# The router's weights as the stationary operand in four column quarters, and a block transpose on VectorE

## The chip, the cores and the metric

The kernel runs on one core of a Trainium2 chip. TensorE multiplies, ScalarE and VectorE work on its results, GpSimd and SyncE issue transfers beside what else they do. The metric is the device time of one execution in microseconds; for the kernel before, it is the median of three runs.

## What is computed

One block of a transformer over 16 sequences of 100 tokens with 256 channels: cross-attention to a context of 361 rows with 16 heads of 64, then a mixture of experts. Only the router is touched by the change, so it is shown in full and the rest in outline:

```python
x = x + cross_attention(layernorm(x), ctx)           # Wq, Wkv, Wproj, bproj
h = layernorm(x)                                     # 1600 tokens x 256
logits = clip(h @ router_w.T + routing_bias, -50, 50)   # router_w: 7 x 256
probs = sigmoid(logits)
p, sel = top_k(probs, 1)                             # one of 7 experts for each token
p = clip(p, 1e-8, 1 - 1e-8)
total = clip(0.5 + p + 1e-8, 0.5, 2.0)
shared = swiglu(h, sw1, sw2, sw3)                    # 704 hidden units
switched = p * swiglu(h, ew1[sel], ew2[sel], ew3[sel])
x = x + 0.5 / total * shared + switched / total
```

Everything is in float32.

## The kernel before

The 1600 tokens lie in 13 tiles of 128 (the last holds 64). `acc` holds them token by token, 128 tokens on the partitions; `xT` holds the normalised tokens turned, 128 channels on the partitions and two halves `k` of the 256 channels, so that matmuls can contract over channels. The tiles are handled in four `GROUPS` of 3, 3, 3 and 4 tiles.

**Attention** (L454 to L848) runs in 32 steps, two for each sequence, 8 heads in each. A step computes scores (L618), their maxima and exponentials, turns the exponentials in blocks of 32 on VectorE (L647), moves the blocks by DMA (L668), and multiplies with the values of the step before (L689). Between the scores stand the products of keys and values for the next sequence (L551), the queries (L527, emptied by VectorE on L534) and the projection (L716). The order of TensorE is written out by hand everywhere; that of ScalarE, VectorE and SyncE is so within the attention, and left to a planner outside it. GpSimd's order is the planner's.

When all tokens of a group are through the attention, the group's norm is computed, its `xT` is made by TensorE transposes (L202, copied on L205), and its router follows. This is done through queues of small parts: `part()` takes one part from `norms` at a time between other work, and `fillers` puts `router(g)` in. So the first three calls of the router, each for 3 tiles, lie inside the attention: behind a step's scores and ahead of query matmuls. The fourth call, for 4 tiles, stands behind the attention, between the second matmuls of the shared expert (`down`, L445 and L448) for one tile and for the next two.

**The router** has, for every tile and each half `k`, one matmul (L232): the 128x128 block of `xT` is the stationary operand and the router's weights, 128 channels by 7 experts, stream through. The logits come out token by token, in one PSUM bank for the whole group, as `lp[token, tile, expert]`. VectorE adds the bias (L246), which takes them out of PSUM, and some twenty small operations give the chosen expert (`onehot`, L273), its probability and the weights of the two sums.

**Behind the fourth call** `sort_tokens` (L294) places every token in a slot of an expert's tile of 128. Its two matmuls (L299, L300) read `onehot`. While VectorE does the sorting, TensorE computes the shared expert's hidden units (L402) for the other groups. Then each expert tile is gathered, multiplied (L920, L929, L941) and scattered to the output; the experts' weights, 2.2 MB a tile, are fetched up to four tiles ahead.

PSUM is used as eight banks of 128x512 that `bank()` hands out in turn. The router's weights `rw_sb` and bias `rb_sb` are loaded in step 3 (L496, L497), far ahead of their first use.

Of the kernel before, what the change touches and what calls it, by code (L numbers as in the profile page):

```python
# [14 lines left out]
F32 = mybir.dt.float32  # L15
# [3 lines left out]
ALU = mybir.AluOpType  # L19
# [6 lines left out]
I, E = 704, 7  # L26
P = 128
# [27 lines left out]
def xattn_moe(  # L55
# [16 lines left out]
    nc = tc.nc  # L72
# [4 lines left out]
    const = ctx.enter_context(tc.tile_pool(name="const", bufs=1))  # L77
    small = ctx.enter_context(tc.tile_pool(name="small", bufs=2))
# [6 lines left out]
    xT = const.tile([P, 2, NT * P], F32, name="xT")  # L85
# [1 line left out]
    ident = const.tile([P, P], F32, name="ident")  # L87
    power = const.tile([P, 4], F32, name="power")
    rank = const.tile([P, E], F32, name="rank")
    rw_sb = const.tile([P, 2, E], F32, name="rw_sb")  # L90
    rb_sb = const.tile([P, E], F32, name="rb_sb")
    bp_sb = const.tile([P, C], F32, name="bp_sb")
    onehot = const.tile([P, NT, E], F32, name="onehot")
# [21 lines left out]
    def bank():  # L115
        return ps.tile([P, 512], F32, tag="mm", name="mm")
# [10 lines left out]
    def load_x(g):  # L127
        full = [t for t in g if t < NT - 1]
        t0, n = full[0], len(full)
        nc.sync.dma_start(  # L130
            acc[:, t0 : t0 + n, :],
            x[t0 * P : (t0 + n) * P, :].rearrange("(t p) c -> p t c", p=P),
        )
        if g[-1] == NT - 1:
            nc.sync.dma_start(acc[:LAST, NT - 1, :], x[(NT - 1) * P :, :])

    make_identity(nc, ident)
    nc.gpsimd.memset(power, -0.5)
    for e in range(E):
        nc.gpsimd.memset(rank[:, e : e + 1], float(E - e))  # L140
        nc.gpsimd.memset(tri[:, e, :], 0.0)
        if e:
            nc.gpsimd.memset(tri[:, e, :e], 1.0)
# [69 lines left out]
    def load_shared(i):  # L213

        if i < 4:
            k, o = i // 2, ds(i % 2 * I, I)
            nc.sync.dma_start(w13_sb[:, k, o], w13[ts(k, P), o])
        elif i == 4:
            nc.sync.dma_start(w2_sb[:, :3, :], w2[: 3 * P].rearrange("(i p) c -> p i c", p=P))
        else:  # L220
            r = w2[3 * P : NI * P].rearrange("(i p) c -> p i c", p=P)
            nc.sync.dma_start(w2_sb[:, 3:NI, :], r)
            nc.sync.dma_start(w2_sb[P - HALF :, NI, :], w2[NI * P :])

    def router(tiles):


        t0, n = tiles[0], len(tiles)
        lp = bank()[:, : 4 * E].rearrange("p (t e) -> p t e", e=E)
        for i, t in enumerate(tiles):  # L230
            for k in range(2):
                nc.tensor.matmul(  # L232
                    lp[:, i, :], xT[:, k, ts(t, P)], rw_sb[:, k, :], start=(k == 0), stop=(k == 1)
                )

        def over_experts(a):
            return a[:, :n].unsqueeze(2).to_broadcast([P, n, E])

        lg = small.tile([P, 4, E], F32, name="lg")
        pr = small.tile([P, 4, E], F32, name="pr")  # L240
        eq = small.tile([P, 4, E], F32, name="eq")
        sat = small.tile([P, 4, E], F32, name="sat")
        top = small.tile([P, 4], F32, name="top")
        tw = small.tile([P, 4], F32, name="tw")
        bias = rb_sb.unsqueeze(1).to_broadcast([P, n, E])
        nc.vector.tensor_tensor(lg[:, :n], lp[:, :n], bias, ALU.add)  # L246
        lmax = small.tile([P, 4], F32, name="lmax")

        def odds():
            nc.vector.tensor_scalar(lg[:, :n], lg[:, :n], -50.0, 50.0, ALU.max, ALU.min)  # L250
            nc.scalar.activation(pr[:, :n], lg[:, :n], AF.Exp, scale=-1.0)
            nc.vector.tensor_scalar(pr[:, :n], pr[:, :n], 1.0, None, ALU.add)
            nc.vector.reciprocal(pr[:, :n], pr[:, :n])

        def best():


            nc.vector.tensor_reduce(top[:, :n], pr[:, :n], AX.X, ALU.max)
            nc.vector.tensor_tensor(eq[:, :n], pr[:, :n], over_experts(top), ALU.is_equal)
            nc.vector.tensor_scalar(sat[:, :n], lg[:, :n], 6.0, None, ALU.is_gt)  # L260
            nc.vector.tensor_tensor(sat[:, :n], sat[:, :n], eq[:, :n], ALU.mult)

        def first():
            nc.vector.tensor_reduce(lmax[:, :n], lg[:, :n], AX.X, ALU.max)
            nc.vector.tensor_tensor(eq[:, :n], lg[:, :n], over_experts(lmax), ALU.is_equal)
            nc.vector.tensor_tensor(eq[:, :n], eq[:, :n], sat[:, :n], ALU.max)
            nc.vector.tensor_tensor(
                eq[:, :n], eq[:, :n], rank.unsqueeze(1).to_broadcast([P, n, E]), ALU.mult
            )
            nc.vector.tensor_reduce(lmax[:, :n], eq[:, :n], AX.X, ALU.max)  # L270

        def chosen():
            nc.vector.tensor_tensor(  # L273
                onehot[:, t0 : t0 + n, :], eq[:, :n], over_experts(lmax), ALU.is_equal
            )
            if tiles[-1] == NT - 1:
                nc.vector.memset(onehot[LAST:, NT - 1, :], 0.0)

        def weights():

            nc.vector.tensor_scalar(top[:, :n], top[:, :n], 1e-8, 1.0 - 1e-8, ALU.max, ALU.min)
            nc.vector.tensor_scalar(tw[:, :n], top[:, :n], 0.5, 1e-8, ALU.add, ALU.add)
            nc.vector.tensor_scalar(tw[:, :n], tw[:, :n], 0.5, 2.0, ALU.max, ALU.min)
            nc.vector.reciprocal(tw[:, :n], tw[:, :n])
            nc.vector.tensor_scalar(coef[:, t0 : t0 + n], tw[:, :n], 0.5, None, ALU.mult)
            nc.vector.tensor_tensor(
                entry[:, t0 : t0 + n, 1], top[:, :n], tw[:, :n], ALU.mult
            )
            if tiles[-1] == NT - 1:
                nc.vector.memset(entry[LAST:, NT - 1, :], 0.0)  # L290

        return [odds, best, first, chosen, weights]
# [161 lines left out]
    with ExitStack() as attn:  # L454
# [33 lines left out]
        def load_later(s):  # L488

            if 1 < s < 4:  # L490
                m = ts(s - 2, NCH // 2)
                nc.sync.dma_start(
                    wp_sb[:, m], wproj.rearrange("(m p) c -> p m c", p=P)[:, m]
                )
            if s == 3:
                nc.sync.dma_start(rb_sb, rbias.to_broadcast([P, E]))  # L496
                nc.sync.dma_start(rw_sb, rwT.rearrange("(k p) e -> p k e", p=P))  # L497
            if s == 4 or s == 7:
                load_x(GROUPS[s // 3 + 1])
            if s == 6 or s == 9:  # L500
                normalised(GROUPS[s // 3])
            if 10 <= s < 16:
                load_shared(s - 10)
# [221 lines left out]
        def normalised(g, keep=False):  # L725
            parts, turn = layer_norm(g, keep)
            norms.extend(parts)
            norms.append(lambda: turns.append(turn))
            if keep:
                norms.append(lambda: fillers.append(lambda: norms.extend(router(g))))  # L730
# [49 lines left out]
        for s, (b, g) in enumerate(steps):  # L780
# [51 lines left out]
            if g == NG - 1 and b + 2 < B:  # L832
                cTs[b + 2] = load_ctx(b + 2)
            load_later(s)
        while first:
            first.pop(0)()
# [51 lines left out]
    with tc.tile_pool(name="hs", bufs=1) as hs:  # L888
        def run_hidden(g):
            n = sum(map(rows, g))  # L890
            hT = hs.tile([P, NI + 1, n], F32, name=f"hT{n}")
            for piece in hidden(g, hT, sp):
                piece()
            return hT

        parts, turn_last = layer_norm(GROUPS[-1], keep=True)
        for one in parts:
            one()
        hT = run_hidden(GROUPS[1])
        turn_last()  # L900
        down(GROUPS[1][:1], hT)
        for one in router(GROUPS[-1]):
            one()
        down(GROUPS[1][1:], hT[:, :, P:])
        fill = sort_tokens(hs)
        for k in range(NW):
            fetch(k)
        hT2 = run_hidden(GROUPS[2])
        fill()
        for k in range(NX - 1):  # L910
            gather_into(xgs, xn_d, k)
        hT3 = run_hidden(GROUPS[3])
        down(GROUPS[2], hT2)
        down(GROUPS[3], hT3)
# [72 lines left out]
    n = nc.values_load(e_at[:, NS:], min_val=0, max_val=NS - NF)  # L987
# [58 lines left out]
```

## Time and profile before

| | |
|---|---|
| median of 3 runs | 731.54 us (731.47 to 731.96) |
| the profiled execution | 730.98 us |
| its span, first to last instruction | 729.3 us |
| granted TensorE clock, mean | 0.998 |
| router matmuls (L232) | 52 matmul records and 52 weight loads, 205.1 to 548.9 us |
| bias addition (L246) | 4 times, 143 to 188 ns |
| load of the router's weights (L497) | issued on SP at 80.9 us |

The profile was taken on one execution. Its engines are PE (TensorE's matmuls), PEld (its weight loads, which overlap the matmuls), DVE (VectorE), ACT (ScalarE), POOL (GpSimd) and SP (SyncE). A line of a group reads: source line, engine, operation, result<-operands, shapes, count, busy time in us and mean ns of one, and the idle time of the engine ahead of it. A line of the timeline has start and length in us in front, and the idle time with its releaser in brackets. A line of a wait reads: who waited <- for whom, us in all, times, longest. A matmul's end is modelled, so its length is not the time after which the next one can start; that is read from the starts.

### The profile page before, as it was taken

The page shows a single profiled execution, that of the slowest core. Times are in us where ns is not written, and L with a number is a line of the kernel's source. Part 1 is how long each engine was busy: PE and PEld are TensorE (multiplying, and loading weights), DVE is VectorE, ACT ScalarE, POOL GpSimd, SP SyncE. Part 2 cuts the span into 40 slices and gives each one's busy share as a digit, 9 for nine tenths or more (in the row PEclk, how much of TensorE's full clock was granted, in tenths as well). Part 3 has the DMA queues.
Part 4 walks back from the last instruction along what each step waited for, and adds up shares of the span by engine and source line. Part 5 has one row for each costly group of instructions (what it writes and reads, how often), then busy time and mean ns, then how long its engine had stood idle before and what let it go on. Part 6 is the DMA issues. An engine that isn't in the chain of part 4 may idle for free. (4 is left out here: it accounts for less than half of the span.)

```text
span 729.3 us, 14750 instructions
## 1 busy us (share of the span) xinstructions
PE 721.5 (99%) x5206; PEld 516.7 (71%) x5206; DVE 421.2 (58%) x1086; ACT 280.3 (38%) x795; POOL 201.7 (28%) x418
## 2 busy tenths in 40 slices
PE   9999999999999999999999999999999999999996
PEld 6667666676666767576676666756767678999996
DVE  2877668568786866857866695776247222222221
ACT  2554556344544544534534463453021101112111
POOL 5242322323323222422223322223020102543221
PEclk9999999999999999999999999999999999999999
DMA  7164655534655553644534554445103901888860
GB/s 256 47 153 113 178 138 134 129 98 127 174 148 126 147 134 85 162 111 126 137 85 126 119 157 111 109 97 121 58 26 109 419 32 48 317 334 344 308 255 23
DMA packets 54375, 107.95 MB, mean 148 GB/s; under 512 B 28631, under 2 KB 35930, under 8 KB 52368
## 3 DMA queue, kind: packets, MB, share of 16 engines
q1 hardware_dynamic: 43648, 80.51, 36.4%
q0 software_dynamic: 10352, 25.98, 14.2%
q8 instruction: 44, 0.72, 0.4%
q14 instruction: 43, 0.35, 0.2%
q10 hardware_dynamic: 288, 0.39, 0.2%
HBM read 60.39 MB, written 5.35 MB: 90 GB/s over the span
## 5 line engine op out<-in xcount | busy, mean ns | idle before, releaser
L634 ACT ACTIVATE at<-mm,nm 128x361 f32<-128x361 f32 x256 | 142.1, 561 | 206.8 <-DVE nm L631 206.6
L668 POOL DMA_DIRECT2D aT<-tb x256 | 126.4, 501 | 300.1 <-PE mm L689 168.4
L631 DVE TENSOR_REDUCE nm<-mm 128x1 f32<-128x361 f32 x256 | 124.0, 526 | 50.9 <-PE mm L618 49.7
L647 DVE STREAM_TRANSPOSE tb<-at 128x384 f32<-128x384 f32 x256 | 132.9, 558 | 4.8 <-DMA aT<-tb 0.6
L551 PE MATMUL mm<-wv_sb,cT 64*128 64x512 f32 (+1 forms) x576 | 131.6, 589 | 0.0
L551 PE MATMUL mm<-cT,wk_sb 64*128 64x361 f32 x768 | 128.4, 465 | 0.0
L551 PEld LDWEIGHTS mm<-cT,wk_sb 64*128 64x128 f32 x768 | 76.3, 188 | 41.4 <-issue 0.5
L618 PE MATMUL mm<-kT,qT 64*128 64x361 f32 x512 | 103.1, 478 | 0.0
L551 PEld LDWEIGHTS mm<-wv_sb,cT 64*128 64x128 f32 (+1 forms) x576 | 53.9, 181 | 57.3 <-issue 46.5
L929 PE MATMUL mm<-xgT,wex 128*128 128x128 f32 x660 | 78.3, 275 | 0.5 <-ACT xgT L922 0.5
L929 PEld LDWEIGHTS mm<-xgT,wex 128*128 128x128 f32 x660 | 76.9, 192 | 1.4 <-issue 0.7
L689 PEld LDWEIGHTS mm<-aT,v 128*64 128x64 f32 (+1 forms) x1536 | 68.9, 135 | 10.6 <-issue 10.6
L689 PE MATMUL mm<-aT,v 128*64 128x100 f32 (+1 forms) x1536 | 75.2, 252 | 0.0
L618 PEld LDWEIGHTS mm<-kT,qT 64*128 64x128 f32 x512 | 46.6, 185 | 38.7 <-issue 14.4
L402 PE MATMUL mm<-xT,w_sb 128*128 128x384 f32 (+1 forms) x176 | 60.9, 503 | 0.0
L402 PEld LDWEIGHTS mm<-xT,w_sb 128*128 128x128 f32 x176 | 32.9, 190 | 25.7 <-issue 8.5
L634 ACT ACTIVATION_READ_ACCUMULATOR at<-mm,nm 128x1 f32 x256 | 50.4, 197 | 0.0
L527 PE MATMUL mm<-xT,wq_sb 128*128 128x200 f32 x256 | 47.2, 337 | 0.7 <-ACT xT L205 0.7
L716 PE MATMUL mm<-wp_sb,resT 128*128 128x256 f32 (+1 forms) x208 | 47.8, 383 | 0.0
L527 PEld LDWEIGHTS mm<-xT,wq_sb 128*128 128x128 f32 x256 | 43.0, 190 | 4.7 <-issue 2.0
L716 PEld LDWEIGHTS mm<-wp_sb,resT 128*128 128x128 f32 (+1 forms) x208 | 37.7, 186 | 9.9 <-ACT at L634 2.5
L941 PE MATMUL mm<-wex,hgT 128*128 128x256 f32 x180 | 41.4, 380 | 0.0
(139 smaller groups left out, 555.2 us busy)
## 6 DMA issues: line engine op xcount, KB each, us to landing
wex<-in_wex SPq DMA_DIRECT2D x15, 2176.0 KB
aT<-tb POOLq DMA_DIRECT2D x256, 80.2 KB, 3.1
aT<-tb SPq DMA_DIRECT2D x256, 80.2 KB
cT<-in_ctxT SPq DMA_DIRECT2D x15, 541.5 KB
over<-row SPq DMA_DIRECT2D x64, 100.0 KB
xn_d<-xn SPq DMA_DIRECT2D x12, 128.0 KB
base_d<-acc SPq DMA_DIRECT2D x12, 128.0 KB
w_sb<-in_w SPq DMA_DIRECT2D x4, 352.0 KB
```

Source lines behind the costliest of these rows:

```text
L402: nc.tensor.matmul(to[:, :n], w13_sb[:, k, ds(at, P)], xT[:, k, ds(g[0] * P, n)], start=(k == 0), stop=(k == 1),)
L527: nc.tensor.matmul(pq[:, o, :], wq_sb[:, u, k, ts(o, P)], xT[:, k, ts(g, QG * LQ)], start=(k == 0), stop=(k == 1),)
L551: nc.tensor.matmul(to[o][:height, :width], *operands(o, k), start=(k == 0), stop=(k == NR - 1),)
L618: nc.tensor.matmul(sc[o][:, :LKV], qTs[b // QG][r, c, ts(b % QG, QB), :], kTs[b][c // 4][r, c % 4, :], start=True, stop=True,)
L631: nc.vector.tensor_reduce(nm[:, o : o + 1], sc[o][:, :LKV], AX.X, ALU.max, negate=True)
L634: nc.scalar.activation(at[:, o, :LKV], sc[o][:, :LKV], AF.Exp, bias=nm[:, o : o + 1], accum_out=sums[:, o : o + 1],)
L647: nc.vector.transpose(tb[:, :, :, o, i * QR : i * QR + 32].rearrange("p j k n -> p k j n"), at[:, o, :].rearrange("p (k j n) -> p k j n", ...
L668: queue.dma_start(aT[ts(j, 32), i].rearrange("p k o n -> p (k o n)"), tb[ts(i, 32), j].rearrange("p k o n -> p (k o n)"),)
L689: nc.tensor.matmul(av[ts(o, DK), i, :], vs[b][:n, j, ds((2 * c + o) * DK, DK)], aT[:n, :, j, o, ts(i, QR)], start=(j == 0), stop=(j == NJ ...
L716: nc.tensor.matmul(pp[:r, :C], resT[:, c, QP : QP + r], wp_sb[:, c, :], start=(c == 0), stop=(c == NCH - 1))
L929: nc.tensor.matmul(to[:, ts(o, P)], w[:, ds(j * 2 * I + u, P)], xgT[:, j, :], start=(j == 0), stop=(j == 1),)
L941: nc.tensor.matmul(y[:, :C], hT[:, c, :], w[:, ds(4 * I + c * C, C)], start=(c == 0), stop=(c == NI))
```

## The change

The operands of the router's matmuls change places. The weights, padded with zeros from 7 to 32 columns (`rw_sb` is cleared by GpSimd at the start and then loaded in part), become the stationary operand, and the tokens run through. For each half `k` there are four matmuls, one for each `q`: the q-th runs of 32 tokens of all tiles of the group are streamed (96 columns, or 128 in the last call) and the result goes to the 32 PSUM partitions from 32q on, so that each matmul lies in another quarter of the array's columns. Now the logits stand expert by expert: in quarter q, expert e on partition 32q + e, tokens along the row. One VectorE transpose in blocks of 32 out of PSUM puts them back token by token into a new SBUF tile `lp`, of which the bias addition reads the first 7 of each 32. What follows is as before.

```diff
-    rw_sb = const.tile([P, 2, E], F32, name="rw_sb")
+    rw_sb = const.tile([P, 2, 32], F32, name="rw_sb")
...
     nc.gpsimd.memset(power, -0.5)
+    nc.gpsimd.memset(rw_sb, 0.0)
...
         t0, n = tiles[0], len(tiles)
-        lp = bank()[:, : 4 * E].rearrange("p (t e) -> p t e", e=E)
-        for i, t in enumerate(tiles):
-            for k in range(2):
+
+        lt = bank()[:, : n * 32]
+        for k in range(2):
+            of = xT[:, k, ds(t0 * P, n * P)].rearrange("p (t q r) -> p q t r", q=4, r=32)
+            for q in range(4):
                 nc.tensor.matmul(
-                    lp[:, i, :], xT[:, k, ts(t, P)], rw_sb[:, k, :], start=(k == 0), stop=(k == 1)
-                )
+                    lt[ts(q, 32), :].rearrange("p (t r) -> p t r", r=32),
+                    rw_sb[:, k, :],
+                    of[:, q],
+                    start=(k == 0),
+                    stop=(k == 1),
+                )
+
+        lp = small.tile([P, 4, 32], F32, name="lp")
+        nc.vector.transpose(lp[:, :n].rearrange("p t e -> p (t e)"), lt)
...
-        nc.vector.tensor_tensor(lg[:, :n], lp[:, :n], bias, ALU.add)
+        nc.vector.tensor_tensor(lg[:, :n], lp[:, :n, :E], bias, ALU.add)
...
-                nc.sync.dma_start(rw_sb, rwT.rearrange("(k p) e -> p k e", p=P))
+                nc.sync.dma_start(rw_sb[:, :, :E], rwT.rearrange("(k p) e -> p k e", p=P))
```

## The prediction

> **What bounds the kernel now.** I read the busy times first, then what the matmul engine waited for, then the groups of the router's line, then the timeline around each router call.
>
> ```profile
> PE 721.5 (99%) x5206; PEld 516.7 (71%) x5206; DVE 421.2 (58%) x1086; ACT 280.3 (38%) x795; POOL 201.7 (28%) x418
> ```
>
> Busy matmuls alone prove little, because their ends are modelled. The waits of PE settle it: these three are all of them, 2.3 us in 729.3.
>
> ```profile
> PE mm L122 <- DVE ones L119: 1.1, 1, 1.1
> PE mm L527 <- ACT xT L205: 0.7, 1, 0.7
> PE mm L929 <- ACT xgT L922: 0.5, 1, 0.5
> ```
>
> So TensorE is the path from start to end, and time taken off its stream comes off the end unless a wait behind it opens. The first question is how much of that stream the router holds. The windows on its line are the stretches from its first matmul to the first matmul of the next line: us, PE busy (instructions), PEld busy (instructions).
>
> ```profile
> 205.13:206.49 1.36, 1.36 (x12) 1.36 (x12) 1.00 0.76 302
> 333.27:334.63 1.36, 1.36 (x12) 1.36 (x12) 1.00 0.09 35
> 456.74:458.10 1.36, 1.36 (x12) 1.36 (x12) 1.00 0.15 57
> 547.30:549.01 1.71, 1.70 (x16) 1.70 (x15) 1.00 0.08 29
> ```
>
> Four calls, 5.79 us at full clock. Each f32 matmul of the source shows as two passes, each with its weight load: 26 matmuls, 52 passes, 111 ns from start to start. Only 7 columns stream in a pass; PEld is as full as PE, so what is paid is the load of 128 weight columns. The nearest rows for the new form are the values matmuls on L689, which already use the array in two column halves:
>
> ```profile
> 208.78 0.67 PE L527 MATMUL mm<-xT,wq_sb 128*128 128x200 f32 x3
> 209.38 2.16 PEld L689 LDWEIGHTS mm<-aT,v 128*64 128x64 f32 x48 [0.24 <-issue]
> 209.38 2.35 PE L689 MATMUL mm<-aT,v 128*64 128x100 f32 x48
> 211.66 0.30 PEld L618 LDWEIGHTS mm<-kT,qT 64*128 64x128 f32 x4
> ```
>
> The reader is to see 48 passes of 100 columns between 209.38 and 211.66. By the single starts in the trace they come in pairs 5 to 7 ns apart, one in each half, and a new pair every 88 ns: the halves run beside each other.
>
> **The price of a pass and of a change of form.** L527 with 200 columns repeats every 169 ns, L445 with 256 every 216: 0.84 ns a column. With L689's 88 ns for 100 columns, 96 columns take 84.5 ns and 128 columns 111 ns. Where the tile form changes (L527 to L689, L689 to L618, L618 to L232), the next start is late by about 92 ns (L527 to L689: 262 ns where a pass is 169), and the first pass of the new form also shows its weight load: 142 ns instead of 88 for 64 weight columns (53), 273 instead of 169 for 128 (105). For 32 columns I estimate 27 from these two.
>
> **Matmuls: removed and added.** Removed: 12 passes (16 for the last group) of 111 ns. The first pass behind the router is also slow (L527 252 ns instead of 169, L445 299 instead of 216), since a stream bound by loads leaves no weights ready: 83 ns. So a call costs 1.36 + 0.08 = 1.44 us, the last 1.70 + 0.08 = 1.79.
>
> Added: 2 halves of the contraction by 4 quarters by 2 passes are 16 passes a call, 64 in all, more than the 52 removed, each with 32 weight columns and 96 or 128 streaming. If the four quarters run side by side, a call is 4 pass times. The first three calls come behind L618, which has another form today too, so the change on entry is paid already; the change on exit, to L527, is new: 4 x 84.5 + 27 + 92 + 105 = 562 ns. The last stands between L445 and L445, so both changes are new: 92 + 27 + 4 x 111 + 92 + 105 = 760 ns. The gain is 3 x 0.88 + 1.03 = 3.67 us; I take 3.6, as four starts 5 to 7 ns apart need a little more than two.
>
> **A rule against it.** The trace's row first: behind the first pair, L689's weight loads start 2 ns after the matmul pair in front of them, on the same 128 rows, and the 88 ns cadence leaves no room for 53 ns of loading in the open. The Trainium skill, "TensorE: Matmul & The Clock Gate", Part 3, section "The mechanism", says that weight loads overlap running matmuls only where the row group differs, and that matmuls are strictly in order. All four quarters share all rows here, so by the rule each pass would show its 27 ns: three more of them a call, 12 x 27 = 0.32 us, and a gain of 3.3. I go by the trace; the rule sits inside the range.
>
> **VectorE.** Each call adds one transpose of 128x96 (last: 128x128) out of PSUM. No row has that. From below: the copy out of PSUM on L302, 128x91, 253 ns; from above: L647's transpose of 128x384 in 558 ns, four times the size. I take 0.26 and, with L977's 292 ns for 128x128 out of PSUM, 0.29. The bias addition now reads SBUF; its 145 ns could move by some 40 either way (L259, the same size from SBUF, 182). Together 1.1 us on VectorE. What hides it:
>
> ```profile
> 207.79 0.15 DVE L246 TENSOR_TENSOR lg<-mm,rb_sb 128x21 f32<-128x21 f32 x1
> 208.13 0.58 DVE L534 TENSOR_SCALAR qT<-mm 128x400 f32<-128x400 f32 x1 [0.19 <-PE mm L527]
> 209.49 0.58 DVE L534 TENSOR_SCALAR qT<-mm 128x400 f32<-128x400 f32 x1 [0.78 <-PE mm L527]
> ```
>
> Queued behind the addition is L534, which empties the query banks, with 0.19 + 0.78 us idle around it (0.71 + 0.78 in the second and third call). TensorE will be 0.88 us earlier and eats part of this, so VectorE trails by about half a microsecond once. The banks are eight and TensorE waits for none here, and the queries of L534 are read more than 2 us later. Without that cover 0.26 us a call would show, 1.1 us in all. I cost it at nothing.
>
> The last call is the tight one, since the sort is on its tail:
>
> ```profile
> 549.19 0.19 DVE L246 TENSOR_TENSOR lg<-mm,rb_sb 128x28 f32<-128x28 f32 x1 [1.20 <-PE mm L232]
> 551.88 0.48 DVE L448 SCALAR_TENSOR_TENSOR acc<-mm,coef,acc 128x256 f32<-128x256 f32 x1 [1.46 <-PE mm L445]
> 554.09 0.06 DVE L277 MEMSET onehot<- 64x7 f32 x1
> 554.22 0.30 PEld L299 LDWEIGHTS mm<-onehot,below 128*128 128x128 f32 x2 [0.18 <-DVE onehot L277]
> ```
>
> From the addition VectorE works until 550.4 and then stands 1.46 us for L448, which waits for TensorE; only behind it comes the chain that ends in the one-hot table at 554.15, for which TensorE waits 0.18 us. The transpose and an addition that starts 0.9 us sooner lie ahead of L448, inside that 1.46; the chain behind moves with TensorE. So 0.18 us of wait stays, and the 1.03 us gets through.
>
> **GpSimd and DMA.** One memset of 64 columns: between 46 columns on L509 (127 ns) and 128 on the identity (198), say 0.14 us, early in GpSimd's queue. Behind it are the query-buffer memsets (until 9.54) and the power for the first norm at 9.65; VectorE's normalised rows end at 11.16, and TensorE, busy with the keys, takes up their transposes at 12.57. The 1.4 us between hide it; without them it would cost 0.14. The load of the router's weights still issues one DMA of 28-byte rows on SP at 80.9 us and is needed at 205: nothing. It now waits for that memset, done 70 us before.
>
> **Sum.** The profiled execution took 730.98 us (span 729.3, 1.7 around it); less 3.6 that is 727.4. The median of the runs is 731.54, 0.56 above that execution, so I forecast 731.54 - 3.6 = 727.9. About 0.2%, 1.5 us, is what a measurement of this kernel can tell from no change.
>
> **Rivals.**
> *Two quarters at a time.* The trace shows two column groups beside each other, never four. Then a call has 8 pass times: 3 x 0.34 + 0.44 = 1.46 us given back, gain 2.1, 729.4. Against: the pairs start 5 ns apart with no sign of a shared limit. Chance 0.10.
> *One after the other (slower).* The quarters are issued with all rows in common, and if the array takes a quarter only after the last, its load included, a call has 16 passes of 84.5 + 27 (or 111 + 27): 1.78 + 0.20 = 1.98 us against 1.44, and for the last 2.40 against 1.79: +2.2 us, 733.7. It decides once a call needs more than about ten pass times with their loads. Against it: L689. Chance 0.10; with the loads hidden it is +0.7, 732.2, chance 0.04.
> *The sort becomes late.* Outside the attention VectorE's order is not written by hand. If the transpose or the addition lands behind L448, the 1.24 us up to the reciprocal and the transpose come on top of the chain to the one-hot table and TensorE waits 1.5 us at L299: gain 2.1, 729.4. For: 0.18 us wait today, no slack. Against: the chain before L448 is ready first. Chance 0.06.
> *Four side by side*, the forecast: 0.69, 727.2 to 728.6. A remaining 0.01 for anything else.
>
> **The numbers.** Faster by over 0.2% holds the forecast, most of the two-at-a-time case and of the late sort: 0.82. Within 0.2%: loads hidden one after the other, and the rest of these: 0.08. Slower: 0.10. The range 727.1 to 730.2 holds the forecast, the rule's 728.2 and both cases at 729.4.
>
> **What would show it.** The router's passes should start in fours within 25 ns, a new four every 85 ns (111 in the last call), and its windows shrink from 1.36 to about 0.46 us up to the next line's start, 1.71 to about 0.56 (the first start itself 92 ns later than now). PE's waits should stay near 2.3 us; a transpose of about 0.26 us should stand before L246's addition. Fours 170 ns apart, or single starts 85 ns apart, would refute the forecast; a wait of over 1 us before L299 would be the sort.

## The result, and the profile after

| | before | after |
|---|---|---|
| median of 6 runs each | 731.50 us (730.51 to 731.96) | 728.14 us (727.90 to 728.37) |
| ratio, 95% interval | | 0.9956 (0.9943 to 0.9969) |
| the profiled execution | 730.98 us | 727.98 us |
| its span | 729.3 us | 726.2 us |

The kernel is faster by 3.4 us; the forecast of 727.9 was 0.2 us off, and the interval of the ratio lies wholly beyond the 0.2% that the prediction took as no change. The new lines lie ten further down than the old ones: L527 became L537, L445 became L455, L448 became L458, L277 became L287, L299 became L309, L689 became L699. The router's matmuls are now L235 (before L232), the transpose L244, the bias addition L256 (before L246).

First the page's row of busy times, and the waits of PE.

```profile
PE 718.0 (99%) x5218; PEld 512.4 (71%) x5218; DVE 422.1 (58%) x1090; ACT 279.6 (39%) x795; POOL 201.3 (28%) x419
```

```profile
PE mm L122 <- DVE ones L119: 1.1, 1, 1.1
PE mm L537 <- ACT xT L206: 0.7, 1, 0.7
PE mm L939 <- ACT xgT L932: 0.5, 1, 0.5
PE mm L951 <- issue: 0.3, 1, 0.3
```

There are 12 more matmul passes than before and PE is busy 3.5 us less. The waits are the same three, with 0.3 us at issue in addition (in "issue" time the engine waited for nothing that the profile shows). No wait came up behind the router, so the time taken off TensorE's stream could come off the end. The windows on the router's line, from its first matmul to the first of the next line (us, PE busy, PEld busy, clock, DMA share, GB/s), fell from 1.36 and 1.71 us to a third of that:

```profile
205.06:205.53 0.47, 0.47 (x16) 0.32 (x16) 1.00 0.98 370
332.32:332.79 0.47, 0.47 (x16) 0.32 (x16) 1.00 0.44 175
454.91:455.38 0.47, 0.47 (x16) 0.32 (x16) 1.00 0.09 37
544.69:545.26 0.57, 0.57 (x16) 0.37 (x16) 1.00 0.00 0
```

The tile view of the router's weights and of `lp` gives the forms (ns min/median/max):

```profile
L235 PEld LDWEIGHTS mm<-xT,rw_sb x64: 106/110/110, 205.1 to 545.0; 128*32 128x32 f32 x64
L235 PE MATMUL mm<-xT,rw_sb x64: 246/246/297, 205.1 to 545.1; 128*32 128x96 f32 x48, 128*32 128x128 f32 x16
L139 POOL MEMSET rw_sb<- x1: 145/145/145, 1.6 to 1.6; 128x64 f32 x1
```

```profile
L244 DVE STREAM_TRANSPOSE lp<-mm x4: 239/246/317, 207.7 to 545.4; 128x96 f32<-128x96 f32 x3, 128x128 f32<-128x128 f32 x1
L256 DVE TENSOR_TENSOR lg<-lp,rb_sb x4: 182/182/190, 208.0 to 545.8; 128x21 f32<-128x21 f32 x3, 128x28 f32<-128x28 f32 x1
```

A matmul that is listed with 246 ns would make 16 of them 3.9 us; they took 0.47. A matmul's end is modelled, so the cadence must be read from the starts. Three stretches of the timeline show it for the first call: up to 0.04 us behind the first start, with the weight loads; up to 0.29 us behind it; and the line that follows the call.

```profile
205.06 0.14 PEld L235 LDWEIGHTS mm<-xT,rw_sb 128*32 128x32 f32 x6 [0.51 <-issue]
205.06 0.29 PE L235 MATMUL mm<-xT,rw_sb 128*32 128x96 f32 x4
```

```profile
205.06 0.53 PE L235 MATMUL mm<-xT,rw_sb 128*32 128x96 f32 x15
```

```profile
205.53 0.60 PE L537 MATMUL mm<-xT,wq_sb 128*128 128x200 f32 x2
```

Four start in the first 0.04 us and 15 in the first 0.29. By the single starts of the trace the four quarters start 6 to 7 ns apart, 20 ns from first to last; the second four comes 107 ns after the first, and each one behind it after 82.5 ns. In the last call, with 128 columns, the distances are 134 and then 109 ns. The last start of a call and the first of L537 are 176 ns apart, and L537's first pass takes 273 ns instead of 169.

How much did a call give back? The cleanest measure is the time from the last matmul start ahead of the router to the third matmul start behind it, which holds the entry, the call, the exit and the slow first pass, and nothing else of the 730 us:

| call | before | after | difference |
|---|---|---|---|
| first | 2176 ns | 1304 ns | -872 |
| second | 2175 | 1303 | -872 |
| third | 2176 | 1303 | -873 |
| last | 2434 | 1419 | -1015 |

The sum is -3.632 us; the prediction had 3 x 0.88 + 1.03 = 3.67. The two spans differ by 3.0 us only, because TensorE lost about 0.65 us in the expert phase of this one profile (622.0 to 623.5 us; 0.3 us of it is the wait at issue above). In a profile of the same kernel taken again that loss was missing. The first microseconds differ too: the 201st matmul pass, long before the router, starts at 38.3 us in the profile before, at 38.2 in this one, at 38.7 in the one taken again, and between 37.6 and 39.1 in all that were kept. From that pass to the end, the one taken again is 3.7 us shorter than the kernel before. A single span carries such accidents of half a microsecond and more, so below I use the sum over the four calls for what the matmuls do, and medians and ratios for the time.

On VectorE, the first call and the last:

```profile
207.72 0.25 DVE L244 STREAM_TRANSPOSE lp<-mm 128x96 f32<-128x96 f32 x1
208.01 0.18 DVE L256 TENSOR_TENSOR lg<-lp,rb_sb 128x21 f32<-128x21 f32 x1
```

```profile
545.40 0.32 DVE L244 STREAM_TRANSPOSE lp<-mm 128x128 f32<-128x128 f32 x1
545.75 0.19 DVE L256 TENSOR_TENSOR lg<-lp,rb_sb 128x28 f32<-128x28 f32 x1
546.66 0.33 DVE L263 RECIPROCAL pr<-pr 128x28 f32<-128x28 f32 x1
548.16 0.48 DVE L458 SCALAR_TENSOR_TENSOR acc<-mm,coef,acc 128x256 f32<-128x256 f32 x1 [1.17 <-PE mm L455]
550.36 0.06 DVE L287 MEMSET onehot<- 64x7 f32 x1
550.49 0.30 PEld L309 LDWEIGHTS mm<-onehot,below 128*128 128x128 f32 x2 [0.18 <-DVE onehot L287]
```

Transpose, addition and reciprocal lie ahead of L458, which waits 1.17 us for TensorE where it waited 1.46; the 0.3 us between is about what the transpose adds. TensorE's wait ahead of the sort stayed 0.18 us. That is the cover that the prediction named for the last call.

### The profile page after: what moved, and what is told of

Its sections match the earlier page's. It is cut to its first block, busy times and chain, and to the rows that moved or that the text cites. A ratio compares the mean times of both kernels' runs of the same rounds, so it can differ in the third digit from the quotient of the medians.

```text
span 726.2 us, 14780 instructions
## 1 busy us (share of the span) xinstructions
PE 718.0 (99%) x5218; PEld 512.4 (71%) x5218; DVE 422.1 (58%) x1090; ACT 279.6 (39%) x795; POOL 201.3 (28%) x419
## 5 line engine op out<-in xcount | busy, mean ns | idle before, releaser
L699 PEld LDWEIGHTS mm<-aT,v 128*64 128x64 f32 (+1 forms) x1536 | 68.9, 135 | 10.6 <-issue 10.6
L699 PE MATMUL mm<-aT,v 128*64 128x100 f32 (+1 forms) x1536 | 75.2, 252 | 0.0
L628 PEld LDWEIGHTS mm<-kT,qT 64*128 64x128 f32 x512 | 46.7, 185 | 38.7 <-issue 14.4
L537 PE MATMUL mm<-xT,wq_sb 128*128 128x200 f32 x256 | 47.2, 337 | 0.7 <-ACT xT L206 0.7
L537 PEld LDWEIGHTS mm<-xT,wq_sb 128*128 128x128 f32 x256 | 43.0, 190 | 5.1 <-issue 2.0
L726 PEld LDWEIGHTS mm<-wp_sb,resT 128*128 128x128 f32 (+1 forms) x208 | 37.7, 186 | 9.9 <-ACT at L644 2.5
```

The lines of the kernel that those rows point to most:

```text
L537: nc.tensor.matmul(pq[:, o, :], wq_sb[:, u, k, ts(o, P)], xT[:, k, ts(g, QG * LQ)], start=(k == 0), stop=(k == 1),)
L628: nc.tensor.matmul(sc[o][:, :LKV], qTs[b // QG][r, c, ts(b % QG, QB), :], kTs[b][c // 4][r, c % 4, :], start=True, stop=True,)
L699: nc.tensor.matmul(av[ts(o, DK), i, :], vs[b][:n, j, ds((2 * c + o) * DK, DK)], aT[:n, :, j, o, ts(i, QR)], start=(j == 0), stop=(j == NJ ...
L726: nc.tensor.matmul(pp[:r, :C], resT[:, c, QP : QP + r], wp_sb[:, c, :], start=(c == 0), stop=(c == NCH - 1))
```

## The experiments

Four theories stand against each other. *Side by side* (the prediction's): the quarters' passes run beside each other, their weight loads hidden, and TensorE is the whole path. *Operand swap*: what helps is that 7 streamed columns were replaced by 96, with no regard to quarters. *Program order*: the four run beside each other only because the quarter changes from one instruction to the next. *VectorE matters*: what was added on VectorE shows, or would show with little more. The edits are shown against the kernel after; times and ratios are against the kernel before, run on the same chip.

**The same kernel again**, with three of the others on one chip.

> The changed kernel again, beside the other runs of this set on one chip: 728.1 us, 3.4 below the kernel before. It is the mark for the others. If the gain were chance of the first measurement, it would shrink towards 731.5.

Measured: 727.97 us against 732.12 before, ratio 0.9946 (0.9933 to 0.9960), and again -3.632 us over the four calls. Of the two sets, one gives 3.2 us by its ratio (0.44% of 731.5), the other 4.0; the traces' 3.63 lies between.

**The operands swapped, but the array used whole.** The weights lie at columns 96 to 102 of a zeroed tile, and a slice of 128 of it places them in quarter q, the rest of the stationary operand being zeros that are added in. The same 16 passes of the same tokens. For want of SBUF, `lp` lies in a tile that is in use elsewhere at other times.

```diff
-    rw_sb = const.tile([P, 2, 32], F32, name="rw_sb")
+    rw_sb = const.tile([P, 2, 224], F32, name="rw_sb")
...
-                    lt[ts(q, 32), :].rearrange("p (t r) -> p t r", r=32),
-                    rw_sb[:, k, :],
+                    lt.rearrange("p (t r) -> p t r", r=32),
+                    rw_sb[:, k, ds(96 - 32 * q, P)],
                     of[:, q],
-                    start=(k == 0),
-                    stop=(k == 1),
+                    start=(k == 0 and q == 0),
+                    stop=(k == 1 and q == 3),
...
-        lp = small.tile([P, 4, 32], F32, name="lp")
+        lp = number.bitcast(F32).rearrange("p (t e) -> p t e", e=32)
...
-                nc.sync.dma_start(rw_sb[:, :, :E], rwT.rearrange("(k p) e -> p k e", p=P))
+                nc.sync.dma_start(rw_sb[:, :, 96 : 96 + E], rwT.rearrange("(k p) e -> p k e", p=P))
```

> The operands stay swapped, but the weights are 128 columns wide, zero outside the quarter's 32, so every matmul fills the whole array and all eight of a call add up in one region; no change of form is left. Theory (the gain is the quarters running side by side): 16 passes one after another, each bound by loading 128 weight columns or by 128 streamed ones, 111 ns: 1.86 us instead of 1.44 for three tiles, about 1.8 for four, so 1.3 us slower than the kernel before, 732.8 us. Rival (the swap itself brings the gain, as tokens now stream through few weights): about 728.5.

Measured: 732.54 us, ratio to before 1.0009 (1.0002 to 1.0015). The calls took +446, +448, +446 and 0 ns more than before: +1.34 us. Its tile view, with weight loads of 128 columns:

```profile
L235 PEld LDWEIGHTS mm<-xT,rw_sb x64: 186/192/192, 205.3 to 550.4; 128*128 128x128 f32 x64
L235 PE MATMUL mm<-xT,rw_sb x64: 273/275/350, 205.3 to 550.5; 128*128 128x96 f32 x48, 128*128 128x128 f32 x16
```

Single starts are 111 to 112 ns apart, as in the kernel before. The timed loss is 0.66 us (0.15 to 1.1), less than the 1.34 of the trace; why the time lost less I did not find. The sign is settled: swapping the operands alone loses, since 16 passes bound by their loads cost more than 12. So the operand swap is not what pays.

**Two halves of 64 columns instead of four quarters.** The weights stand twice in zeroed tiles of 64 columns, at column 0 and at column 32, so two quarters of the tokens are added up in each half.

```diff
-    rw_sb = const.tile([P, 2, 32], F32, name="rw_sb")
+    rw_sb = const.tile([P, 2, 2, 64], F32, name="rw_sb")
...
-            for q in range(4):
-                nc.tensor.matmul(
-                    lt[ts(q, 32), :].rearrange("p (t r) -> p t r", r=32),
-                    rw_sb[:, k, :],
-                    of[:, q],
-                    start=(k == 0),
-                    stop=(k == 1),
-                )
+            for j in range(2):
+                for h in range(2):
+                    nc.tensor.matmul(
+                        lt[ts(h, 64), :].rearrange("p (t r) -> p t r", r=32),
+                        rw_sb[:, k, j, :],
+                        of[:, 2 * h + j],
+                        start=(k == 0 and j == 0),
+                        stop=(k == 1 and j == 1),
+                    )
...
-                nc.sync.dma_start(rw_sb[:, :, :E], rwT.rearrange("(k p) e -> p k e", p=P))
+                for j in range(2):
+                    nc.sync.dma_start(
+                        rw_sb[:, :, j, 32 * j : 32 * j + E], rwT.rearrange("(k p) e -> p k e", p=P)
+                    )
```

> The weights are 64 columns wide, in two column halves, two quarters of the tokens added up in each half. Theory: two passes at a time, so 8 pass times a call: 8 x 84.5 + 53 + 92 + 105 = 0.93 us instead of 1.44 in the first three calls, 92 + 53 + 8 x 111 + 92 + 105 = 1.23 instead of 1.79 in the last: 2.1 us faster than before, 729.4 us, with starts in pairs. Rival (the swap itself): about 728.5, the same as with quarters. If halves did not overlap at all: about 732.5.

Measured: 729.10 us, ratio 0.9964 (0.9954 to 0.9975). The calls differ from before by -529, -528, -529 and -565 ns: -2.15 us.

```profile
L236 PEld LDWEIGHTS mm<-xT,rw_sb x64: 132/137/137, 205.1 to 546.4; 128*64 128x64 f32 x64
L236 PE MATMUL mm<-xT,rw_sb x64: 246/246/323, 205.1 to 546.5; 128*64 128x96 f32 x48, 128*64 128x128 f32 x16
```

Starts come in pairs, a new pair every 82.5 ns. The cadence of a group is the same for two and for four at a time; only the number of groups differs, eight against four. The three kernels with 16 passes a call form a ladder by what runs beside each other: one (+1.34), two (-2.15), four (-3.63). The profile does not say in which quarter a pass lies, and no run put all narrow passes on one quarter, so that a narrow stationary operand shortens its pass wherever it lies was not tested by itself. Against it: the starts come in groups as large as the number of column groups, and the groups lie 82.5 ns apart, about what L527's 0.84 ns a column makes of one stream of 96 (81 ns, an estimate).

**The kernel before, with the transpose alone.** The old matmuls, the weights padded to 32 streamed columns, and the transpose into a tile that nobody reads.

```diff
-        for k in range(2):
-            of = xT[:, k, ds(t0 * P, n * P)].rearrange("p (t q r) -> p q t r", q=4, r=32)
-            for q in range(4):
+        lp = lt.rearrange("p (t e) -> p t e", e=32)
+        for i, t in enumerate(tiles):
+            for k in range(2):
                 nc.tensor.matmul(
-                    lt[ts(q, 32), :].rearrange("p (t r) -> p t r", r=32),
-                    rw_sb[:, k, :],
-                    of[:, q],
-                    start=(k == 0),
-                    stop=(k == 1),
+                    lp[:, i, :], xT[:, k, ts(t, P)], rw_sb[:, k, :], start=(k == 0), stop=(k == 1)
                 )
-        lp = small.tile([P, 4, 32], F32, name="lp")
-        nc.vector.transpose(lp[:, :n].rearrange("p t e -> p (t e)"), lt)
+        spare = small.tile([P, 4, 32], F32, name="lp")
+        nc.vector.transpose(spare[:, :n].rearrange("p t e -> p (t e)"), lt)
```

> The kernel before, with the router's weights padded to 32 streamed columns and the block transpose added on VectorE into a tile that nobody reads; the matmuls stay as they were. Theory: 32 columns stream within the 111 ns that a weight load takes anyway and the transposes lie beside TensorE's work: no change, 731.5 us within 0.3. Rival (the transpose is on the path and the change earned more than it shows): 4 x 0.26 = 1.1 us slower, 732.6.

Measured: 731.69 us against 732.12, ratio 0.9993 (0.9985 to 1.0001), and at most 1 ns of difference in any call.

```profile
L234 PE MATMUL mm<-rw_sb,xT x52: 192/276/297, 205.9 to 549.7; 128*128 128x32 f32 x52
```

The transposes are hidden. By their single starts these passes are 111 to 112 ns apart, as with 7 columns, and as with the 96 of the whole-array form: a pass with 128 weight columns is paid by its load.

**The quarter as the outer loop**, with the same matmuls: two halves `k` of a quarter now follow each other in the program.

```diff
-        for k in range(2):
-            of = xT[:, k, ds(t0 * P, n * P)].rearrange("p (t q r) -> p q t r", q=4, r=32)
-            for q in range(4):
+        of = xT[:, :, ds(t0 * P, n * P)].rearrange("p k (t q r) -> p k q t r", q=4, r=32)
+        for q in range(4):
+            for k in range(2):
...
-                    of[:, q],
+                    of[:, k, q],
```

> As the changed kernel, but the quarters are the outer loop and the halves of the contraction the inner one, so four passes of one quarter follow each other in the program. Theory (each quarter takes its passes on its own, and a pass waits only for the one before it in its quarter): fours every 83 ns as before, 728.1 us. Rival (starts go in the order of the program, with at most one pass of a quarter waiting): a quarter starts only when the third pass of the one in front has started, 10 pass times a call instead of 4: 3 x 0.50 + 0.65 = 2.1 us slower than the changed kernel, 730.3 us.

Measured: 727.58 us against 731.34, ratio 0.9943 (0.9930 to 0.9956); -3.552 us over the calls. The timeline's line of the first call:

```profile
205.67 0.56 PE L235 MATMUL mm<-xT,rw_sb 128*32 128x96 f32 x16
```

Fours still come every 82.5 ns; within a four the starts are 13 to 14 ns apart instead of 6 to 7, and that is the 20 ns more that a call takes. Program order is refuted, for two matmuls of a quarter in a row.

**Every matmul of the router twice.**

```diff
-        for k in range(2):
+        for k in (0, 1, 0, 1):
```

> The eight matmuls of each router call are issued twice into the same region. Theory: a second set costs four pass times and no change of form: 3 x 0.33 + 0.44 = 1.4 us more than the changed kernel, 729.5 us. If a pass cost its weight load in the open too, 27 ns each: 1.9 us more, 730.0.

Measured: 729.59 us, ratio 0.9972 (0.9960 to 0.9984); -2.205 us over the calls, so 1.43 us more than the kernel after. The price of the 64 added passes is 16 pass times, three calls at 4 x 82.5 and one at 4 x 109: 1.43. Doubled work measures the cadence without entry and exit, and it is a quarter of what 64 passes at 82.5 and 109 ns would cost one after the other.

**A matmul of the old form in the middle of a call**, to price a change of form.

```diff
+            if k == 0:
+                nc.tensor.matmul(
+                    bank()[:, :E], xT[:, 0, ts(t0, P)], rw_sb[:, 0, :E], start=True, stop=True
+                )
```

> Between the two halves of the contraction stands one small matmul on the whole array (128 weight columns, 7 streamed, its result unused), so the form of the array changes two more times a call. Theory: 92 + 160 for its two passes + 92 + 27 = 0.37 us a call, 1.5 us more than the changed kernel, 729.6. If changing the form cost nothing, only its passes: 0.6 us, 728.7.

Measured: 729.86 us, ratio 0.9981 (0.9974 to 0.9989); 0.455 us more in a call than the kernel after, where about 0.37 was expected. The timeline of the first call:

```profile
204.73 0.37 PE L235 MATMUL mm<-xT,rw_sb 128*32 128x96 f32 x8
205.04 0.39 PE L243 MATMUL mm<-rw_sb,xT 128*128 128x7 f32 x2
205.35 0.37 PE L235 MATMUL mm<-xT,rw_sb 128*32 128x96 f32 x8
```

From the last start of a four to the small matmul are 176 ns, as to L537 in the kernel after; its two passes then take 132 and 185 ns up to the next four. If the change takes 92 ns here too, 93 ns are left for the second pass, where I had put 28; why is open. One such small matmul of the old form between quarters costs more than the eight passes on either side of it.

**Six more transposes in each call**, to use up VectorE's cover.

```diff
         nc.vector.transpose(lp[:, :n].rearrange("p t e -> p (t e)"), lt)
+        for _ in range(6):
+            nc.vector.transpose(lp[:, :n].rearrange("p t e -> p (t e)"), lt)
```

> The transpose of each call is issued seven times instead of once, 6 x 0.246 us more on VectorE in the first three calls and 6 x 0.317 in the last. Theory: in the first three calls nothing of it reaches TensorE; in the last, 1.9 us stand against 1.17 us in which VectorE now waits for the down product, so the one-hot table is 0.7 us late and TensorE's wait ahead of the sort grows from 0.18 to about 0.9: 728.8 us. Rival (VectorE's work shows in full): 6.3 us more, 734.4.

Measured: 733.30 us against 731.34, ratio 1.0024 (1.0018 to 1.0031). This is 4.5 us over the 728.8 that I expected. The matmuls of the calls were as fast as ever (-3.632 us), so the loss lies in waits. Those of PE that are new:

```profile
PE mm L311 <- DVE onehot L289: 2.4, 1, 2.4
...
PE mm L701 <- ACT at L646: 0.9, 1, 0.9
```

There are 0.2 us more at L701 for a DMA. This is VectorE behind the fourth call (lines stand two further down than in the kernel after):

```profile
547.39 2.07 DVE L246 STREAM_TRANSPOSE lp<-mm 128x128 f32<-128x128 f32 x6
549.50 0.19 DVE L258 TENSOR_TENSOR lg<-lp,rb_sb 128x28 f32<-128x28 f32 x1
549.80 0.48 DVE L460 SCALAR_TENSOR_TENSOR acc<-mm,coef,acc 128x256 f32<-128x256 f32 x1
550.88 0.33 DVE L265 RECIPROCAL pr<-pr 128x28 f32<-128x28 f32 x1
552.39 0.48 DVE L460 SCALAR_TENSOR_TENSOR acc<-mm,coef,acc 128x256 f32<-128x256 f32 x1 [1.19 <-PE mm L457]
554.59 0.06 DVE L289 MEMSET onehot<- 64x7 f32 x1
554.72 0.30 PEld L311 LDWEIGHTS mm<-onehot,below 128*128 128x128 f32 x2 [2.77 <-DVE onehot L289]
```

The order has changed: one down product's addition (L460) now stands ahead of the reciprocal, and the choice of the expert comes behind the last one. That is the prediction's "sort becomes late", brought about by force, and at 2.4 us instead of 1.5. A third part is the clock. The windows around it (us, PE, PEld, DVE, ACT, POOL, clock, DMA share, GB/s):

```profile
552.00:554.70 2.70, 0.35 (x2) 0.00 (x0) 2.14 (x17) 0.00 (x0) 0.41 (x1) 1.00 0.14 49
554.70:557.40 2.70, 2.68 (x9) 1.81 (x10) 1.75 (x7) 0.01 (x1) 0.00 (x0) 0.74 0.02 6
557.40:559.50 2.10, 2.10 (x4) 1.05 (x4) 1.56 (x12) 1.77 (x2) 0.00 (x0) 0.52 0.00 0
559.50:562.00 2.50, 2.50 (x9) 1.52 (x8) 2.05 (x7) 0.49 (x1) 0.00 (x0) 1.00 0.35 84
```

Behind the 2.4 us stand-still the granted clock fell to about half for 3.4 us, which cost another 1.7 us (0.26 of 2.70 us and 0.48 of 2.10). Of this kernel's 21 runs 16 had a mean clock of 0.997 or less, at about 733.5 us, and the other five were at about 732.4. From its 201st matmul pass to the end this profile is 5.5 us longer than that of the kernel after taken again. Less the 1.7 of the clock that is 3.8, which on top of the 727.6 of the run with the quarter as outer loop makes 731.4, an estimate; so about 1 us of those five stays unexplained.

Three more kernels take this apart: the six transposes in the first three calls only, two in the last only, and six in the last only.

```diff
-        for _ in range(6):
+        for _ in range(6 if n < 4 else 0):
```

> The six extra transposes stand in the first three calls only, the last call is that of the changed kernel. In the run with them in all calls TensorE waited 0.9 us for ScalarE ahead of the values matmuls after the second call, and 0.3 us after the third. Theory (the attention has about 0.6 us of cover for VectorE there, not 1.5): 1.2 us more than the changed kernel, about 729.0. Rival (nothing of it is the first three calls): 727.8.

Measured: 729.24 us against 731.29, ratio 0.9972 (0.9961 to 0.9983): 1.3 us of the gain gone, as expected. The profile (of the shortest of its runs, with an early start: its 201st pass is at 37.7 us) shows 0.93 us lost at the values matmuls behind the second call, 0.33 behind the third and nothing behind the first; the wait and the larger one in the timeline:

```profile
PE mm L701 <- DMA over<-row: 1.1, 2, 0.9
```

```profile
348.35 0.90 PE L701 MATMUL mm<-aT,v 128*64 128x100 f32 x15 [0.86 <-DMA over<-row]
```

What VectorE is late with there is the turning of the exponentials, whose blocks go through a DMA to the values product: the last of that step (L659) ends at 338.46 us, and the DMA of its rows is on its way from 338.48. About 1.5 us of transposes cost 0.93 us there, so the cover in the attention is, at its tightest, some 0.5 us beyond what the change uses; at the queries, which the prediction looked at, no wait came up.

```diff
-        for _ in range(6):
+        for _ in range(0 if n < 4 else 2):
```

> Two extra transposes, in the last call only: 0.64 us, less than the 1.17 us in which VectorE waits there. By the time alone they are free: 727.8. But in the program's order the down product's addition now comes ahead of the reciprocal and the operation before it, which moves 0.4 us of the chain to the one-hot table behind it: theory, TensorE's wait ahead of the sort grows from 0.18 to about 0.6 us, 728.3.

Measured: 727.75 us (727.24 to 728.22), ratio 0.9951 (0.9937 to 0.9964). The time can't tell half a microsecond here. The profile can: PE's wait ahead of the sort, and the order on VectorE.

```profile
PE mm L311 <- DVE onehot L289: 0.4, 1, 0.4
```

```profile
548.70 0.48 DVE L460 SCALAR_TENSOR_TENSOR acc<-mm,coef,acc 128x256 f32<-128x256 f32 x1 [1.01 <-PE mm L457]
549.30 0.33 DVE L265 RECIPROCAL pr<-pr 128x28 f32<-128x28 f32 x1
```

Two transposes, 0.6 us, are enough to put the addition of L460 ahead of the reciprocal, though at a small price: 0.4 us of wait, where about 0.6 was expected.

```diff
-        for _ in range(6):
+        for _ in range(0 if n < 4 else 6):
```

> Six extra transposes, in the last call only. In the program's order VectorE's second step on the logits now stands behind the next down product's addition and the choice of the expert behind the last one. Theory: TensorE waits 2.4 us for the one-hot table and then works for about 3 us at a granted clock of 0.5, which costs another 1.7 us: 4.0 us more than the changed kernel, 731.8. Rival (the clock is no cost of the wait): 2.3 us more, 730.1.

Measured: 730.43 us (729.44 to 731.68), ratio 0.9987 (0.9979 to 0.9996). The wait is there as in all calls' case, the clock loss is not (PE's windows with the clock behind the count):

```profile
PE mm L311 <- DVE onehot L289: 2.4, 1, 2.4
```

```profile
551.50:553.90 2.40, 0.04 (x1) 1.00 0.16 55
553.90:557.30 3.40, 3.40 (x13) 1.00 0.02 5
```

So about 2.4 us is the price of the wait alone, and my number, which had the clock in it, was 1.4 too high. Two of its 13 runs had a mean clock of 0.997 or less, and they are its slowest but one and its slowest, 731.1 and 731.7.

**The wait filled with unused matmuls.** As the last, and five matmuls of 256 columns into a bank that nobody reads, ahead of the sort.

```diff
+        warm = bank()
+        for _ in range(5):
+            nc.tensor.matmul(warm[:, :C], xT[:, 0, :P], w2_sb[:, 0, :], start=True, stop=True)
```

> As the one with six extra transposes in the last call, with five matmuls of 256 columns, whose result nobody reads, ahead of the sort's matmuls: 10 passes of 216 ns fill 2.16 of the 2.4 us in which TensorE would wait. Theory (standing still for over 2 us lowers the granted clock afterwards): the clock stays at 1, 1.7 us less than without them, 730.1 us, although TensorE does more. Rival (the lower clock has another cause): 731.8, as without them.

Measured: 730.38 us, ratio 0.9986 (0.9979 to 0.9992), as without them. The wait fell to 0.3 us, by as much as the matmuls took:

```profile
PE mm L311 <- DVE onehot L289: 0.3, 1, 0.3
```

```profile
549.92 2.32 PE L919 MATMUL mm<-w_sb,xT 128*128 128x256 f32 x10
```

It was to show whether a busy TensorE keeps the clock; since the kernel without them lost no clock either, it says nothing on that. Why the same 2.4 us wait halved the clock in most runs of one kernel and in few of another stays open.

## Why the prediction was right

**What bounds.** TensorE is the path, as its waits had said: -3.63 us in the calls, -3.4 us in the medians, and each of the experiments that changed only the matmuls moved the time with its calls, the whole-array form to its sign only. That the median came within 0.2 us of the forecast is closer than the runs can tell: the two sets put the gain at 3.2 and at 4.0 us.

**Side by side.** The chance of 0.69 lay on the right case. L689's two halves were a sound witness for four: the fours start within 20 ns, and the halves and doubling experiments gave the cadence from two further sides. *Two quarters at a time* and *one after the other* would have shown 165 ns between fours or 82.5 between single starts; neither was there.

**The sum.** A pass of 96 columns was put at 84.5 ns and took 82.5, one of 128 at 111 and took 109. The exposed load of 32 columns was put at 27 and is the 107 - 82.5 = 24.5 ns ahead of the second four. The change of form on exit, put at 92, is the 176 ns to L537 less a pass: 93. L537's first pass is 273 ns, as read from the kernel before. The 20 ns between the first and the last start of a four, which the prediction allowed for in rounding 3.67 to 3.6, are in the sum too: 3.632. The 83 ns that the prediction put behind the old form, for loads that leave no weights ready, also fit: behind the whole-array passes of 96 columns L537's first pass takes 198 ns instead of 169, behind those of 128 columns L455's takes 219 instead of 216, so what is late shrinks as the stream covers more of the 112 ns of the load.

One of the prediction's sums is off, without bearing on the forecast: *one after the other* leaves out the change on entry in the last call, which is 2.50 us then, not 2.40 (733.8), and its break-even lies nearer eleven pass times than ten.

**The rule against it.** In the trace, the second four's weight loads start at 205.088, 26 ns after the first matmul and while the first four run (six loads and four matmuls in the 0.04 us shown above), on the same 128 rows, and fours are 82.5 ns apart, which is less than the 84.5 of the streaming alone. Only the first four's load shows. The rule that the prediction set against L689 (loads hide only where the row group differs) would have given 3.3; this case's quarters give 3.63. It went by the right one of the two. But the section that it took the rule from (the Trainium skill, "TensorE: Matmul & The Clock Gate", Part 3, "The mechanism") also lets a load that goes to the background weight buffer be pulled ahead of running matmuls, and so does not forbid what the trace shows. Strict order of the matmuls, the rule's other half, does not fit the run with the quarter as outer loop: with at most one pass of a quarter waiting it would have cost 2.1 us more over the calls, and 0.08 was measured.

**VectorE.** Transposes of 246 and 317 ns against 260 and 290, an addition of 182 ns where 145 give or take 40 was put: 0.3 us more ahead of L458, inside the wait as foreseen. The transpose-only kernel shows that they cost nothing. The argument for it was weaker than its outcome in two places. In the attention the cover was reckoned from the queries, but what comes late first is the turned exponentials, with about half a microsecond to spare. In the last call, the rival "the sort becomes late" had 0.06; 0.6 us of further VectorE work already changes the order there, and 2 us make it cost 2.4. The prediction named that place rightly, and the cover was real, but narrow.

**GpSimd and DMA.** The memset took 145 ns (0.14 put), at 1.6 us, and nothing waited for it; `rw_sb` has no wait in its tile view, so the load of the weights cost nothing either.

## What to carry to other kernels

Where a stationary operand has few columns that matter, ask whether a pass is paid by its load or by its stream; if by its load, make the narrow operand stationary and let several narrow column groups run beside each other, but only that: the swap without the groups lost time. Cost a call with its entry and exit: here the two changes of form and the slow first pass behind were over two fifths of what is left of it (92, 93 and 104 of some 660 ns), and a single small matmul of another form in its middle cost 0.46 us. When an off-path engine gets new work that a planner orders, look not only at the idle time but at what else the planner may put ahead of it; a forced doubling shows how far the cover reaches.

## What the runs showed of the hardware

- Four column quarters take four streams of 128 rows at once: a new four every 82.5 ns for 96 columns, as a new pair with two halves. Their order in the program matters little, 6 to 7 ns between starts where the quarter changes with every matmul, 13 to 14 where it changes with every second.
- From a 7-column pass to the first pass of another form were 185 ns, 93 more than the 92 of a change; the first two passes of the last call before were 28 ns apart.
- A stand-still of TensorE of 2.4 us was followed in 16 of 21 runs of one kernel by a low mean clock (0.997 or less), in its profile half the clock for 3.4 us (the passes of the hidden units, L414 there, took 640 instead of 322 ns), and in another kernel with the same wait in 2 of 13; kernels without it had such a clock in 4 of 207. So a wait's price can be more than its length, and not in every run.
